# A written order for the first work of all engines: keys and values of group 0 first, then the weight product, and small constants in whole rows

## The chip, the cores and the metric

The kernel runs on one core of a Trainium2 chip. The metric is device time in microseconds (us). A core has five instruction queues that run side by side, each strictly in its own order: TensorE (PE, matmuls and transposes; PEld is its weight load), VectorE (DVE), ScalarE (ACT), GpSimd (POOL), and SyncE (SP), whose queue issues all DMA transfers of this kernel. An instruction waits at the head of its queue until its semaphores are reached, and all that stands behind it waits too.

## The reference, cut to what matters

Two layers over 8 batches of 128 tokens, width 512, all in f32. Layer 0 is a cross-attention with one head, without a mask, followed by a linear layer whose low-rank part is chosen by a gate. Layer 1 is a cross-attention with 32 query heads and 8 key/value groups, and a gated feed-forward network with integer weights. The layers are wired with layer norms and residual sums; `ctx` is the context `ctx_4096`.

```python
# layer 0, attention
Q = einsum('btx,dx->btd', text, Wq) + bq
K = einsum('bpx,dx->bpd', features, Wk) + bk
scores = einsum('btd,bpd->btp', Q, K) / sqrt(512)
attended = einsum('btp,bpd->btd', softmax(scores), features)
# layer 0, linear part with a routed low-rank part (TOPK = 1)
out = einsum('bsd,od->bso', hidden_states, W) + b
scores = x @ gate_w.T + gate_b          # 4 ranks: 8, 16, 32, 64
final = x @ A[:r].T @ B[:, :r].T        # r is the rank that the gate selects
# layer 1, attention: 32 heads, 8 key/value groups, head size 128
q = rmsnorm(x @ q_proj_w.T); k = rmsnorm(ctx @ k_proj_w.T); v = ctx @ v_proj_w.T
# layer 1, feed-forward: integer weights, dequantised by groups of 128
...
```

## The kernel before

**Numbers in two parts.** An f32 operand is split into a rounded high part and the remainder (`_h`, `_l`), and a product takes three matmuls (`mm3`, lines 78 to 80). A split is a cast on ScalarE and a subtraction on VectorE (`split_fast`), a cast on ScalarE and a subtraction on GpSimd (`split_both`), or both on GpSimd (`split_pool`, lines 61 and 62).

**Halves and blocks.** The 1024 tokens are two halves (`hf`) of four blocks of 128 (`HB = 4`). Matrices of 512 rows come in four pieces (`KT = 4`) of 128 x 512.

**Layer 0** does not form Q and K. It forms M = Wq^T Wk once (`weight_product`, 48 matmuls), then per half `proj_T`: the normed tokens times M, four blocks of 12 matmuls into a PSUM pool of two banks (`ps_mm`), each evicted by ScalarE with a bias column `vcol` (line 185). The bias terms need row sums of weight times bias: `vcol` from WkT and `bq`, `ucol` from WqT and `bk`. `ucol` goes to HBM and comes back as a row on all partitions (`u_d`, then `p0T`, lines 366 and 368), where VectorE reduces it (`usum`) and multiplies it with the tokens (line 188). After that come scores (line 232), softmax, the product with the context, a second layer norm, the gate and low-rank part (`ag`, 64 columns of A and 4 of the gate padded to 128, line 278), and the output product with `WT` and `BT`. Both halves run as generators that are advanced in turn.

**Keys and values of layer 1** depend on the context alone: `kv_group(g)` loads group g's weights, splits them and makes four `kv_part`s of 24 matmuls with 256 columns, each followed by Square sums, casts, cuts and a norm; `kv_out` writes them to HBM. Groups 0 to 5 fill TensorE beside layer 0 and before layer 1, groups 6 and 7 go into layer 1's first rounds.

**What sets the order.** All of this stands in the part of the program that a scheduler orders by its own cost estimates. From layer 1's rounds on (line 944) the order is written out by hand. Waits at most eight transfers deep are seen in SyncE's queue: each DMA waits for the one eight before it. The loads at the start are issued in the scheduler's order: Wq and Wk, x, bq, WkT, x, bk, WqT, small constants (lines 375 to 381), the context, and so on. The tables `gsT`, `usT`, `dsT` (lines 918 to 920) are read in pieces of 16 and 56 bytes, the gate's columns in pieces of 16 bytes.

Of the kernel before, what the change touches and what calls it, by code (L numbers as in the profile page):

```python
# [34 lines left out]
def f32(ap):  # L35
    return ap.bitcast(F32)
# [3 lines left out]
def tile_layers(ctx: ExitStack, tc: tile.TileContext, t, out: bass.AP):  # L40
# [36 lines left out]
    def mm3(o, ah, al, bh, bl, start, stop):  # L77
        nc.tensor.matmul(o, ah, bl, start=start, stop=False)  # L78
        nc.tensor.matmul(o, ah, bh, start=False, stop=False)  # L79
        nc.tensor.matmul(o, al, bh, start=False, stop=stop)  # L80
# [88 lines left out]
    gb = w0.tile([P, 4], F32, name="gb")  # L169
    ag = w0.tile([P, KT, P], F32, name="ag")  # L170

    bTh, bTl = (w0.tile([P, D], F32R, name=f"bT_{p}") for p in "hl")
    nc.vector.memset(ag[:, :, 68:128], 0.0)
    scale0 = 1.0 / math.sqrt(D)

    def proj_T(w, src, bias, dst):
        for j in range(KT):
            ps = ps_mm.tile([P, TOK], F32, name="mm")
            cols = slice(j * P, (j + 1) * P)
            for k in range(KT):  # L180
                mm3(
                    ps, w[0][:, k, cols], w[1][:, k, cols], src[0][:, k, :], src[1][:, k, :],
                    k == 0, k == KT - 1,
                )
            nc.scalar.activation(dst[:, j, :], ps, AF.Identity, bias=bias[:, j : j + 1])

    def dot(junk, a, b, o):
        nc.vector.scalar_tensor_tensor(junk, a, 1.0, b, ALU.mult, ALU.mult, accum_out=o)

    def weight_product():  # L190

        wq_, wk_ = wts["WqT"], wts["WkT"]
        pss = [ps_mm.tile([P, D], F32, name="mm") for _ in range(2)]
        pss += [ps_kv.tile([P, 2, 2 * HD], F32, name="kv").rearrange("p a b -> p (a b)") for _ in range(2)]
        for k in range(KT):
            for j, ps in enumerate(pss):
                cols = slice(j * P, (j + 1) * P)
                mm3(
                    ps, wq_[0][:, k, cols], wq_[1][:, k, cols], wk_[0][:, k, :], wk_[1][:, k, :],
                    k == 0, k == KT - 1,  # L200
                )
        mh, ml = (l0.tile([P, KT, D], F32, name="qx", bufs=2).bitcast(F32R) for _ in range(2))
        for j, ps in enumerate(pss):
            split_fast(mh[:, j, :], ml[:, j, :], ps)
        wts["M"] = mh, ml

    def layer0(hf):
        xt = xs[hf]
        xn = layernorm_T(
            hf, ps_tr, keep=lambda b: (mvk[:, hf * HB + b, :], rsk[:, hf * HB + b : hf * HB + b + 1])  # L210
        )
        if hf == 0:
            weight_product()
        yield
        kT = c_st[hf]
        qT = w0.tile([P, KT, TOK], F32R, name="wkf0_" + "hl"[hf]).bitcast(F32)
        proj_T(wts["M"], xn, vcol, qT)
        yield

# [55 lines left out]
        for b in range(HB):  # L275
            cols = slice(b * P, (b + 1) * P)
            for k in range(KT):
                nc.tensor.matmul(
                    agp[:, b, :], xf[:, k, cols], ag[:, k, :], start=(k == 0), stop=(k == KT - 1)
                )  # L280
# [57 lines left out]


    wk_st, wq_st = (l0.tile([P, KT, D], F32, name="qx", bufs=2) for _ in range(2))  # L340
    for k in range(KT):
        rows = slice(k * P, (k + 1) * P)
        nc.sync.dma_start(wq_st[:, k, :], t["Wq"][rows, :])
        nc.sync.dma_start(wk_st[:, k, :], t["Wk"][rows, :])
    for b in range(HB):
        nc.sync.dma_start(xs[0][:, b, :], t["x"][b])
    bq_bc, bk_bc = (l0.tile([P, D], F32R, name=f"cn_{p}", bufs=1).bitcast(F32) for p in "hl")
    wkT_st, wqT_st = (l0.tile([P, KT, D], F32, name="k0T", bufs=2) for _ in range(2))
    nc.sync.dma_start(bq_bc, t["bq"].to_broadcast([P, D]))
    for k in range(KT):  # L350
        nc.sync.dma_start(wkT_st[:, k, :], t["WkT"][k * P : (k + 1) * P, :])
    for k in range(KT):
        for nm, st_ in (("WqT", wq_st), ("WkT", wk_st)):
            split_fast(wts[nm][0][:, k, :], wts[nm][1][:, k, :], st_[:, k, :])
    A, B = layer0(0), layer0(1)
    next(A)
    for k in range(KT):
        dot(wkT_st[:, k, :], wkT_st[:, k, :], bq_bc, vcol[:, k : k + 1])
    for b in range(HB):
        nc.sync.dma_start(xs[1][:, b, :], t["x"][HB + b])  # L360
    nc.sync.dma_start(bk_bc, t["bk"].to_broadcast([P, D]))
    for k in range(KT):
        nc.sync.dma_start(wqT_st[:, k, :], t["WqT"][k * P : (k + 1) * P, :])
        dot(wqT_st[:, k, :], wqT_st[:, k, :], bk_bc, ucol[:, k : k + 1])
    u_d = dram.tile([1, D], F32, name="u_d")
    nc.sync.dma_start(u_d.rearrange("o (k p) -> p (o k)", p=P), ucol)
    u_bc = l0.tile([P, HB, P], F32R, name="p0T").bitcast(F32).rearrange("p b c -> p (b c)")
    nc.sync.dma_start(u_bc, u_d.to_broadcast([P, D]))
    nc.vector.tensor_reduce(usum, u_bc, AX.X, ALU.add)
    c_st = [l0.tile([P, KT, TOK], F32, name="k0T", bufs=2) for _ in range(2)]  # L370
    for hf in range(2):
        for k in range(KT):
            nc.sync.dma_start(c_st[hf][:, k, :], t["ctxT"][k * P : (k + 1) * P, hf * TOK : (hf + 1) * TOK])
            (split_both if hf else split_fast)(cTh[hf][:, k, :], cTl[hf][:, k, :], c_st[hf][:, k, :])
    nc.sync.dma_start(b0, t["ffn_b"].to_broadcast([P, D]))
    nc.sync.dma_start(gb, t["gate_b"].to_broadcast([P, 4]))
    nc.sync.dma_start(ag[:, :, 0:64], t["AT"].rearrange("(k p) r -> p k r", p=P))
    nc.sync.dma_start(ag[:, :, 64:68], t["gwT"].rearrange("(k p) r -> p k r", p=P))
    bs = stage.tile([P, D], F32, name="wstage")
    nc.sync.dma_start(bs[0:64, :], t["BT"])  # L380
    nc.sync.dma_start(bs[64:128, :], t["BT"])
    split_pool(bTh, bTl, bs)
    next(B)
    next(A)
    tile_w0("WT")
    load_w0("WT", split_pool)
    next(B)
    done = False
    order = [A, B]
    while order:  # L390
        for it in list(order):
            try:
                next(it)
            except StopIteration:
                order.remove(it)

    def rms_factor(ssq, n, kind):
# [10 lines left out]
    wkn = const.tile([P, HD], F32, name="wkn")  # L408
    nc.sync.dma_start(wqn, t["qnw"].to_broadcast([P, HD]))
    nc.sync.dma_start(wkn, t["knw"].to_broadcast([P, HD]))  # L410
    nc.vector.scalar_tensor_tensor(wkn, wkn, 1.0 / math.sqrt(HD), wqn, ALU.mult, ALU.mult)
    kT_d, v_d = {}, {}
# [16 lines left out]

    def kv_part(g, hf, b0_):  # L430
        wh, wl = kvw[g]
        if b0_ == 0:
            kvo[g, hf] = (
                kvp.tile([P, HB, HD], F32, name="kn", bufs=1),
                kvp.tile([P, HB, HD], F32R, name="vh"),
                kvp.tile([P, HB, HD], F32R, name="vl"),
            )
        kn, vh, vl = kvo[g, hf]
        ps = ps_kv.tile([P, 2, 2 * HD], F32, name="kv")
        for i in range(2):  # L440
            cols = slice((b0_ + i) * P, (b0_ + i + 1) * P)
            for k in range(KT):
                mm3(
                    ps[:, i, :], cTh[hf][:, k, cols], cTl[hf][:, k, cols], wh[:, k, :], wl[:, k, :],
                    k == 0, k == KT - 1,
                )
        ssq = small.tile([P, 2], F32, name="kssq")
        for i in range(2):
            junk = small.tile([P, HD], F32, name="junk", bufs=2)
            nc.scalar.activation(junk, ps[:, i, 0:HD], AF.Square, accum_out=ssq[:, i : i + 1])  # L450
        bs = slice(b0_, b0_ + 2)
        nc.scalar.copy(vh[:, bs, :], ps[:, :, HD:])
        nc.vector.tensor_tensor(vl[:, bs, :], ps[:, :, HD:], f32(vh[:, bs, :]), ALU.subtract)
        rk = rms_factor(ssq, 2, "k")
        for i in range(2):
            nc.vector.scalar_tensor_tensor(
                kn[:, b0_ + i, :], ps[:, i, 0:HD], rk[:, i : i + 1], wkn, ALU.mult, ALU.mult
            )
# [19 lines left out]

    for g in range(4):
        kv_group(g)  # L480
# [436 lines left out]

    nc.sync.dma_start(sg_sb, t["gsT"].rearrange("(c p) g -> p c g", p=P))
    nc.sync.dma_start(su_sb, t["usT"].rearrange("(c p) g -> p c g", p=P))
    nc.sync.dma_start(sd_sb, t["dsT"].rearrange("(c p) g -> p c g", p=P))  # L920
    for k in range(KT):
# [326 lines left out]
```

## Time and profile before

| what | value |
|---|---|
| median of 3 runs | 849.55 us (848.87 to 850.13) |
| the profiled execution | 851.54 us, span 849.8 us |
| busy: PE, PEld, DVE, ACT, POOL | 816.7, 687.3, 648.1, 514.6, 602.4 us |
| DMA | 167.85 MB, mean 198 GB/s, 155388 packets, 16048 of them under 512 B |
| mean granted TensorE clock | 0.987 of full speed |

The profile shows one execution. Busy time counts from the start of an instruction to its end; matmuls overlap, so a row of 128 x 512 is listed with 0.39 us while one starts every 0.23 us. A row of the timeline has the start, the length, the engine, the line of the code, the operation, `out<-in` by the program's names, shapes, a count, and in brackets the idle time before it with what ended it. `SPq` is SyncE's queue. A row of waits has who waited for whom, the sum in us, how often, and the longest. A row of stretches has the stretch, its length, busy times of PE, PEld, DVE, ACT and POOL with instruction counts, the granted clock of TensorE, the share of DMA engines and GB/s.

### The profile page before, as it was taken

The page shows a single profiled execution, that of the slowest core. Times are in us where ns is not written, and L with a number is a line of the kernel's source. Part 1 is how long each engine was busy: PE and PEld are TensorE (multiplying, and loading weights), DVE is VectorE, ACT ScalarE, POOL GpSimd, SP SyncE. Part 2 cuts the span into 40 slices and gives each one's busy share as a digit, 9 for nine tenths or more (in the row PEclk, how much of TensorE's full clock was granted, in tenths as well). Part 3 has the DMA queues.
Part 4 walks back from the last instruction along what each step waited for, and adds up shares of the span by engine and source line. Part 5 has one row for each costly group of instructions (what it writes and reads, how often), then busy time and mean ns, then how long its engine had stood idle before and what let it go on. Part 6 is the DMA issues. An engine that isn't in the chain of part 4 may idle for free.

```text
span 849.8 us, 14099 instructions
## 1 busy us (share of the span) xinstructions
PE 816.7 (96%) x4264; PEld 687.3 (81%) x4264; DVE 648.1 (76%) x1105; ACT 514.6 (61%) x1687; POOL 602.4 (71%) x615
## 2 busy tenths in 40 slices
PE   6589999999999999999999999999999999999996
PEld 5479999899878888888888888888888866778775
DVE  7843897685677777777777777777798897998987
ACT  4233443245567766676667666677776668765663
POOL 2362784234588877787778778798897778798686
PEclk9789999999999999999999999999999999999998
DMA  9751542073789988888888888988887612232202
GB/s 324 154 149 61 181 148 106 27 241 137 223 287 297 291 273 257 290 256 260 261 272 280 255 258 275 293 270 271 273 256 227 201 36 86 74 87 75 63 25 100
DMA packets 155388, 167.85 MB, mean 198 GB/s; under 512 B 16048, under 2 KB 94640, under 8 KB 155312
## 3 DMA queue, kind: packets, MB, share of 16 engines
q1 hardware_dynamic: 155312, 166.94, 62.0%
q8 instruction: 34, 0.56, 0.3%
q14 instruction: 42, 0.34, 0.2%
HBM read 107.66 MB, written 59.25 MB: 196 GB/s over the span
## 4 chain that ended last, share of the span: by engine, by line
PE 80%; DMA 7%; DVE 4%; issue 3%; POOL 3%; ACT 2%; SPq 1%; POOLq 0%; DVEq 0%; ACTq 0%
PE mm L78 8%; PE mm L80 8%; PE mm L79 8%; PE f L1017 7%; PE o L679 7%; PE f L1018 7%; PE o L680 6%; PE o L682 6%; PE s L610 6%; PE kv L80 3%; PE kv L79 3%; PE kv L78 3%; PE o L659 2%; PE o L658 2%; PE o L660 2%
## 5 line engine op out<-in xcount | busy, mean ns | idle before, releaser
L624 ACT ACTIVATE pr<-s,nm 128x128 f32<-128x128 f32 x256 | 90.6, 366 | 47.6 <-DVE nm L618 45.8
L78 PE MATMUL mm<-wq_l,xnT_h 128*128 128x512 f32 x288 | 118.7, 412 | 0.2 <-DVE q L579 0.2
L80 PE MATMUL mm<-wq_h,xnT_l 128*128 128x512 f32 x288 | 113.8, 395 | 0.0
L79 PE MATMUL mm<-wq_h,xnT_h 128*128 128x512 f32 x288 | 113.5, 394 | 0.0
L651 POOL TENSOR_TENSOR pT_l<-pT,pT_h 128x512 fp32r<-128x512 f32 x64 | 83.0, 1296 | 26.6 <-ACT pT_h L650 26.3
L679 PE MATMUL o<-wo_l,aT_h 128*128 128x512 f32 x256 | 101.3, 396 | 0.3 <-DVE xs L687 0.3
L680 PE MATMUL o<-wo_h,aT_h 128*128 128x512 f32 x256 | 100.3, 392 | 0.0
L632 POOL TENSOR_TENSOR pr<-pr,rs 128x512 f32<-128x512 f32 x64 | 67.8, 1059 | 25.4 <-DVE rs L630 25.1
L636 DVE STREAM_TRANSPOSE pb<-pr 128x512 f32<-128x512 f32 x64 | 45.5, 711 | 48.2 <-POOL pr L632 48.1
L570 ACT ACTIVATE junkq<-mm 128x128 f32<-128x128 f32 x256 | 71.8, 280 | 10.9 <-PE mm L80 4.8
L78 PE MATMUL kv<-wkv_l,cT_h 128*128 128x256 f32 x256 | 73.1, 286 | 0.0
L79 PE MATMUL kv<-wkv_h,cT_h 128*128 128x256 f32 x256 | 73.1, 286 | 0.0
L80 PE MATMUL kv<-wkv_h,cT_l 128*128 128x256 f32 x256 | 73.1, 286 | 0.0
L610 PEld LDWEIGHTS s<-kT,qT 128*128 128x128 f32 x512 | 66.8, 191 | 5.5
L708 POOL TENSOR_TENSOR qT<-qT,q 128x512 fp32r<-128x512 f32 x42 | 54.3, 1292 | 23.8 <-ACT qT L707 23.8
L682 PE MATMUL o<-wo_h,aT_l 128*128 128x512 f32 x256 | 69.0, 391 | 0.0
L401 POOL TENSOR_TENSOR rrq<-msq,nhalf 128x4 f32<-128x4 f32 x64 | 64.6, 1009 | 5.3
L610 PE MATMUL s<-kT,qT 128*128 128x128 f32 x512 | 67.3, 274 | 0.0
L664 ACT CAST aT_h<-o 128x512 fp32r<-128x512 f32 x64 | 37.6, 587 | 48.0 <-PE o L660 47.7
L80 PEld LDWEIGHTS mm<-wq_h,xnT_l 128*128 128x128 f32 x288 | 54.1, 188 | 12.6
L78 PEld LDWEIGHTS mm<-wq_l,xnT_h 128*128 128x128 f32 x288 | 54.5, 189 | 10.0 <-ACT junkq L570 0.4
L79 PEld LDWEIGHTS mm<-wq_h,xnT_h 128*128 128x128 f32 x288 | 54.4, 189 | 9.9
(264 smaller groups left out, 2417.1 us busy)
## 6 DMA issues: line engine op xcount, KB each, us to landing
q_d<-qb SPq DMA_DIRECT2D x64, 256.0 KB, 4.2
qT<-q_d SPq DMA_DIRECT2D x64, 256.0 KB, 4.1
p_d<-pb SPq DMA_DIRECT2D x64, 256.0 KB, 2.5
pT<-p_d SPq DMA_DIRECT2D x64, 256.0 KB, 4.6
wst<-in_qpT SPq DMA_DIRECT2D x36, 256.0 KB, 3.9
wst<-in_opT SPq DMA_DIRECT2D x36, 256.0 KB, 3.1
wkv<-in_kvT SPq DMA_DIRECT2D x8, 512.0 KB, 4.0
v_d<-vh SPq DMA_DIRECT2D x16, 256.0 KB, 2.9
```

The costliest lines, as they stand in the source:

```text
L78: nc.tensor.matmul(o, ah, bl, start=start, stop=False)
L79: nc.tensor.matmul(o, ah, bh, start=False, stop=False)
L80: nc.tensor.matmul(o, al, bh, start=False, stop=stop)
L401: nc.gpsimd.tensor_tensor(r[:, :n], ms[:, :n], nhalf[:, :n], ALU.pow)
L570: nc.scalar.activation(junk, qps[u][:, r * HD : (r + 1) * HD], AF.Square, accum_out=ssq[:, r : r + 1])
L610: nc.tensor.matmul(sp[:, r, :], qTs[u][:, r, :], kTt[blocks[j]][:, :, i, :], start=True, stop=True)
L624: nc.scalar.activation(pr[:, r, :], sps[u][:, r, :], AF.Exp, bias=nms[u][:, r : r + 1], accum_out=sm[:, r : r + 1])
L632: nc.gpsimd.tensor_tensor(pr, pr, rs.unsqueeze(2).to_broadcast([P, NQ, P]), ALU.mult)
L651: nc.gpsimd.tensor_tensor(pl, tps[u], f32(ph), ALU.subtract)
L679: nc.tensor.matmul(po, ah[:, r, :], wl, start=r == 0, stop=False)
L680: nc.tensor.matmul(po, ah[:, r, :], wh, start=False, stop=False)
L682: nc.tensor.matmul(po, al[:, r, :], wo[wset[j], r][0], start=False, stop=r == NREP - 1)
```

## The change

The first part of the program leaves the scheduler and is written in order for every queue (`tc.manual_schedule()`); what comes after it is still ordered by the scheduler, which may put later instructions between those of the written part.

- Group 0's weights and context half 0 are loaded first, piece by piece, and four blocks of keys and values are summed side by side in four banks (three of `ps_kv`, one of `ps_s`). Their evictions (`kv_part` with banks given) come after the first block of the weight product.
- `weight_product` becomes `product(j, ks)`, one output block after the other, with cuts, norms and transposes of half 0 written between them. Two of Wk's cuts move from VectorE to GpSimd.
- The row sums for `vcol` and `ucol` (one VectorE instruction each before) become a GpSimd product (`times`) and a ScalarE sum (`column`).
- Keys and values of group 1 for half 0 start before the first projection. The cuts of context half 1 are written between the projection's evictions. Loads are issued in the written order; `b0`, `gb`, `ag`, `BT`, `WT` come after it.
- `ag` has 68 columns instead of 128 and comes as one table with whole rows; the scale tables `gsT`, `usT`, `dsT` come as whole rows too.

```diff
-    ag = w0.tile([P, KT, P], F32, name="ag")
+    ag = w0.tile([P, KT, 68], F32, name="ag")
...
-                    agp[:, b, :], xf[:, k, cols], ag[:, k, :], start=(k == 0), stop=(k == KT - 1)
+                    agp[:, b, 0:68], xf[:, k, cols], ag[:, k, :], start=(k == 0), stop=(k == KT - 1)
...
-    for k in range(KT):
-        dot(wkT_st[:, k, :], wkT_st[:, k, :], bq_bc, vcol[:, k : k + 1])
...
+    def times(w_st, b_bc, k):
+        nc.gpsimd.tensor_tensor(w_st[:, k, :], w_st[:, k, :], b_bc, ALU.mult)
+
+    def column(w_st, col, k):
+        nc.scalar.activation(w_st[:, k, :], w_st[:, k, :], AF.Identity, accum_out=col[:, k : k + 1])
+
+    with tc.manual_schedule():
+        w0_st = kvw[0] = kvp.tile([P, KT, 2 * HD], F32, name="wkv", bufs=1)
+        for k in range(KT):
+            nc.sync.dma_start(w0_st[:, k, :], t["kvT"][0][k * P : (k + 1) * P, :])
+            load_c(0, k)
...
+        banks = [ps_kv.tile([P, 2, 2 * HD], F32, name="kv")[:, 0, :] for _ in range(3)]
+        banks.append(ps_s.tile([P, HB, P], F32, name="s")[:, 0:2, :].rearrange("p a b -> p (a b)"))
+        for k in range(KT):
+            split_fast(wh[:, k, :], wl[:, k, :], w0_st[:, k, :])
+            split_fast(cTh[0][:, k, :], cTl[0][:, k, :], c_st[0][:, k, :])
+            for b, ps in enumerate(banks):
+                cols = slice(b * P, (b + 1) * P)
+                mm3(ps, cTh[0][:, k, cols], cTl[0][:, k, cols], wh[:, k, :], wl[:, k, :], k == 0, k == KT - 1)
+        kv_load(1)
...
+            split_fast(wq_[0][:, k, :], wq_[1][:, k, :], wq_st[:, k, :])
+            (split_both if k > 1 else split_fast)(wk_[0][:, k, :], wk_[1][:, k, :], wk_st[:, k, :])
...
+        product(0, range(KT))
+
+        nc.vector.scalar_tensor_tensor(wkn, wkn, 1.0 / math.sqrt(HD), wqn, ALU.mult, ALU.mult)
+        for b0_ in (0, 2):
+            kv_part(0, 0, b0_, banks[b0_ : b0_ + 2])
+        stats(0)
+        stats(1)
+        product_cut(0)
+        product(1, range(KT))
...
+        for k in range(KT):
+            column(wkT_st, vcol, k)
+        kv_out(0, 0)
+        for b in range(HB):
+            stats(HB + b)
+        kv_part(1, 0, 0)
...
+        for k in range(KT):
+            times(wqT_st, bk_bc, k)
+            column(wqT_st, ucol, k)
+        normed(HB)
+        normed(HB + 1)
+
+        def second_context(k):
+            split_both(cTh[1][:, k, :], cTl[1][:, k, :], c_st[1][:, k, :])
+
+        proj_T(wts["M"], xnT0[0], vcol, qTs0[0], second_context)
+        nc.sync.dma_start(u_d.rearrange("o (k p) -> p (o k)", p=P), ucol)
...
+        nc.sync.dma_start(u_bc, u_d.to_broadcast([P, D]))
+        turns(HB + 2)
+        turns(HB + 3)
+    proj_T(wts["M"], xnT0[1], vcol, qTs0[1])
+    nc.vector.tensor_reduce(usum, u_bc, AX.X, ALU.add)
+    A, B = layer0(0), layer0(1)
+    nc.sync.dma_start(b0, t["ffn_b"].to_broadcast([P, D]))
+    nc.sync.dma_start(gb, t["gate_b"].to_broadcast([P, 4]))
+    nc.sync.dma_start(ag, t["agT"].rearrange("p (k r) -> p k r", r=68))
...
+    split_pool(bTh, bTl, bs)
+    tile_w0("WT")
+    load_w0("WT", split_pool)
...
+    kv_part(1, 0, 2)
+    kv_out(1, 0)
...
-    nc.sync.dma_start(sg_sb, t["gsT"].rearrange("(c p) g -> p c g", p=P))
+    nc.sync.dma_start(sg_sb, t["gsT"].rearrange("p (c g) -> p c g", g=KT))
...
-        "gsT": g["L1_ffn_gate_s"].T,
+        "gsT": g["L1_ffn_gate_s"].reshape(KT, NI, P).transpose(2, 1, 0).reshape(P, NI * KT),
```

## The prediction

> **What bounds the kernel now.** I read the page first, then TensorE's waits, then the queues of the stage in which it waits.
>
> ```profile
> PE 816.7 (96%) x4264; PEld 687.3 (81%) x4264; DVE 648.1 (76%) x1105; ACT 514.6 (61%) x1687; POOL 602.4 (71%) x615
> ...
> PE   6589999999999999999999999999999999999996
> ```
>
> TensorE is busy in 96% of the span, and the slices that are not full are the first three (64 us). From 60 us on its matmuls follow each other at 0.23 us (512 columns), 0.12 us (256) and 0.11 us (f32, 128). So the time is TensorE's work plus the time that it loses, and nearly all loss is at the start. Its waits in the first 260 us:
>
> ```profile
> PE tr L100 <- DVE xnT_l L107: 7.5, 2, 5.0
> PE mm L78 <- ACT wkf_h L185: 6.5, 2, 6.0
> PE mm L78 <- DVE wkf_l L66: 5.6, 1, 5.6
> ```
>
> To these comes a slow clock after each pause: the stretches show the granted clock behind the busy times.
>
> ```profile
> 20.00:30.00 10.00, 3.06 (x15) 2.17 (x16) 10.00 (x24) 3.25 (x6) 2.38 (x7) 0.64 1.04 275
> ...
> 40.00:50.00 10.00, 5.51 (x14) 4.35 (x15) 0.00 (x0) 2.72 (x5) 2.80 (x3) 0.66 0.60 157
> ```
>
> Counted: up to 38.5 us TensorE did 72 matmuls of 512 columns, 32 transposes and 3 of 256 columns, 16.4 + 3.5 + 0.4 = 20.3 us of work. It goes on at 44.49 us, so 24.2 us are lost; the next 12 matmuls take 5.3 us, not 2.7 (half clock), then 0.45 us of wait and some tenths more: **28.0 us lost by 70 us**, and nothing after that up to 200 us. Who is late is in the DMA queue:
>
> ```profile
> 29.06 0.38 SPq L918 DMA_DIRECT2D sg_sb<-in_gsT  x1
> 29.77 2.99 SPq L919 DMA_DIRECT2D su_sb<-in_usT  x1
> 32.81 1.37 SPq L920 DMA_DIRECT2D sd_sb<-in_dsT  x1
> 34.27 0.45 SPq L366 DMA_DIRECT2D u_d<-ucol  x1
> 34.77 1.93 SPq L373 DMA_DIRECT2D k0T<-in_ctxT  x4
> 36.80 2.17 SPq L74 DMA_DIRECT2D wstage<-in_WT  x2
> 43.07 2.07 SPq L368 DMA_DIRECT2D p0T<-u_d  x1
> ```
>
> The scale tables and u_d are some 4,600 pieces of 4 to 56 bytes; the moved bytes drop from about 300 GB/s to 5 to 44 GB/s between 32.8 and 42.4 us (2.1 ns a piece). Context half 1 lands behind them, ScalarE stands in its queue at that cast, and the eviction that frees TensorE's bank stands behind the cast.
>
> **The change, step by step.** Work on TensorE is the same but for L278. So I compare lost time at two places. The order of instructions in the built kernel shows which queue stands where; durations are rows of the trace before.
>
> *Start.* The first matmul waits for a 128 KB and a 256 KB load and their casts in place of two 256 KB ones: about 4.7 us against 5.55. 48 key and value matmuls (5.7 us, at half clock for about 4 us: 2 lost) lie over the arrival of Wq and Wk. The last of these is the 18th load: 3.8 MB at 345 KB/us (317 fit the loads landed by 29 us, 365 the stretch from 10 to 20 us), 11.0, plus the 2.9 us that one v_d transfer takes from issue to landing: 13.9; then ScalarE 0.62 and GpSimd 1.29, so the first product block ends near 16.6 us with 8.4 us of work done, 8.2 lost. Waits for the first cut (about 1.4) and for transposes (0.9) make 10.5. Before the third block of the first projection TensorE has 96 x 0.119 + 72 x 0.228 + 16 x 0.11 = 29.6 us of work, so it gets there at **40.1 us**.
>
> *The new wait.* That block needs the bank of the first one, freed by ScalarE's eviction. In ScalarE's queue four row sums of Wq's columns stand ahead of it; each waits for GpSimd's product with bk. In GpSimd's queue the splits of BT and of two WT pieces stand ahead of these, and those loads are the last of 45 units of 256 KB: 11.8 MB / 345 = 34.2, plus 2.9: the second WT piece lands at 37.1 us, the first at 36.4. GpSimd from there: 0.62 + 1.3 + 0.6 + 0.2 + 0.62 + 1.3 + 0.7 = 5.3, then four products at 1.29 (the row of the same form below): 47.0.
>
> ```profile
> 53.87 1.29 POOL L62 TENSOR_TENSOR wq_l<-wstage,wq_h 128x512 fp32r<-128x512 f32 x1
> ```
>
> ScalarE's last sum 0.78, eviction 0.68 and a tenth: TensorE goes on at **48.6 us**, 8.5 us late, and at half clock again (2.5, as after the wait of 6.0 before).
>
> *The round trip of u.* The sums are done at 47.8. VectorE's queue holds its reduction of u ahead of all cuts of half 1.
>
> ```profile
> DVE usum L369 <- DMA p0T<-u_d: 13.1, 1, 13.1
> ```
>
> u_d took 8.7 us and the broadcast 8.6 behind other loads; alone the nearest rows are 2.9 plus 512 x 2.1 ns, 4.0, and 3.3 for the broadcast. Bounds together: 5.8 to 17.3; I take 7.3, since the queue is nearly empty then. 55.1; VectorE 0.6 + 6 x 0.68 + 0.5: 60.3; a context load (its stage buffer is freed by these) 2.8; GpSimd 0.62 + 0.6 + 1.3 + 1.29: **66.9 us**, when the last context cut that the next key block needs is there. TensorE's work by then is 29.6 + 11.5 (24 x 0.228, 32 x 0.11, 21 x 0.119) = 41.1, so it has lost 25.8. Against 28.0: **2.2 us gained**.
>
> *The switch of layers.* Group 0 and half of group 1 are used up at the start, so less is left to cover the end of layer 0. Before, TensorE has over 110 key and value matmuls (13 us) between the last output block of layer 0 (174.3 us) and the queries. In the changed order 19 remain. After that last block VectorE has, up to the last query weight: one add 0.6, three normalisations 1.6, statistics 0.7, three cuts 1.8, four weight cuts 2.4, zero points 0.5, value cut and two keys 0.9, a group's weight cuts 1.4, small waits 0.3: 10.2 us. TensorE has 19 x 0.119 + 16 x 0.11 + 9 x 0.228 = 6.1. Lost: 4.1, and the clock. After a pause of 2.55 us at 19 us, eight transposes took 1.43 us, not 1.03: 0.4. **4.5 us lost** (2.5 to 6).
>
> The Trainium skill, "TensorE: Matmul & The Clock Gate", section "Why this matters for your kernels", warns of idle gaps over about 3 us, after which the array runs at half clock. By it the long wait above is charged and this gap of 2 to 3 us is not; the 0.4 would go and the time would be 851.2.
>
> *The rest.* L278 takes 68 columns in place of 128 in 32 matmuls of 0.11: 0 to 1.7 us less. The 256-column row costs 0.12 and the f32 one of 128 columns 0.11, so columns alone do not set the pitch: I take 0.3. The whole-row tables free the DMA stretch above, which is in the start already; nothing else waits for them. The Square, copy and cut of the first values in four pieces, the moved wkn product and the memset lie on ScalarE and VectorE beside TensorE's product: 0 as long as TensorE has the second product block, up to 1 if not (in the 10.5).
>
> *Sum:* -2.2 + 4.5 - 0.3 = **+2.0 us**. The profiled execution took 851.54 us (span 849.8), the median of three runs is 849.55, 2.0 lower; on the profiled one this gives 853.5, on the median **851.6 us**. About 0.2% (1.7 us) is what a measurement here can tell from no change.
>
> **The rivals.**
> 1. *Faster: the switch is covered.* If the queries' weights are cut before VectorE meets the last half's normalisations, only the start counts: 849.55 - 2.2 - 0.3 = 847.1; and if the loads also run at 365 KB/us (TensorE goes on 1.9 us earlier), 845.2. For it: before, there is no loss at the switch at all. Against: VectorE's order is fixed and holds a group's weight cuts ahead of the last query cut. It decides if those 10.2 us become under 6.
> 2. *Slower by the u round trip.* If u_d and its broadcast take 8.7 + 8.6 as before, everything behind VectorE's reduction comes 10 us later: 861.6. For it: u_d still moves 4-byte pieces. Against: the loads that stood ahead of it are gone. From 4 us more it decides (over 855).
> 3. *The start's gain is kept whole:* if BT and WT land before 31 us, the wait at the third block is 2 to 3 us in place of 8.5 and the time 845 to 846. That needs 420 KB/us, above all rows.
>
> **How the numbers follow.** My case 0.6 (own range 848.5 to 855, since the switch is 2.5 to 6, the round trip moves it by 2 and L278 by 1.4), rival 1 0.25, rival 2 0.1, rival 3 0.05. Range for 8 in 10: 845 to 857, which takes in rival 1 and the shorter half of rival 2. Slower by over 0.2%: 0.42 of my case and rival 2, 0.52; within: 0.17 of my case and 0.03 of rival 1, 0.20; faster: the rest, 0.28.
>
> **What would show it.** Right: TensorE waits 7 to 10 us for ScalarE's eviction near 40 us; GpSimd's products of Wq wait for WT; VectorE waits for the broadcast of u until 53 to 58 us; waits for VectorE of 3 to 5 us near 185 us. Wrong: no wait at 40 us (the loads were faster), none at 185 us, or a wait over 5 us near 64 us (rival 2).

## The result and the profile after

The changed kernel took **864.19 us** (863.67 to 866.11, four runs), the kernel before 849.21 us beside it: a ratio of 1.0179 (1.0161 to 1.0197), 15 us slower. Measured again beside the experiments (e13 below) it was 1.0175. Foretold were 851.6 us, between 845 and 857. The sign of the likeliest case was right, the size was not. The profiled execution took 866.11 us, with a span of 864.3 us.

The page of the changed kernel, the busy line and TensorE's slices:

```profile
PE 824.4 (95%) x4264; PEld 691.1 (80%) x4264; DVE 641.5 (74%) x1088; ACT 517.8 (60%) x1705; POOL 611.7 (71%) x625
...
PE   6957999998999999999999999999999999999996
```

Before, the first three slices were not full. Now slices 1, 3 and 4 (to 86 us) are not, and the tenth (194 to 216 us) has an 8. These are the two places of the forecast, the start and the switch of layers. TensorE's waits up to 260 us say for whom it stands there:

```profile
PE mm L78 <- ACT wkf_h L184: 8.0, 1, 8.0
PE kv L80 <- POOL cT_l L70: 7.0, 2, 6.4
PE kv L78 <- ACT cT_h L65: 4.5, 1, 4.5
PE mm L78 <- DVE wq_l L635: 2.3, 1, 2.3
```

The third row is the first matmul (foretold 4.7 us; 5.5 in e13). The first is the foretold wait for ScalarE's eviction (7 to 10 us). The second is the one that the forecast named as the sign of rival 2, a wait of over 5 us near 64 us. The rows of the timeline on its way:

```profile
51.61 0.38 SPq L537 DMA_DIRECT2D u_d<-ucol  x1
62.20 0.32 SPq L544 DMA_DIRECT2D p0T<-u_d  x1
65.33 0.69 DVE L548 TENSOR_REDUCE usum<-p0T 128x1 f32<-128x512 f32 x1 [16.86 <-DMA p0T<-u_d]
66.13 1.88 POOL L200 TENSOR_SCALAR tm<-mvk,usum 128x4 f32<-128x4 f32 x2 [6.88 <-DVE usum L548]
67.98 1.26 POOL L70 TENSOR_TENSOR cT_l<-k0T,cT_h 128x512 fp32r<-128x512 f32 x1
69.29 0.80 PE L80 MATMUL kv<-wkv_h,cT_l 128*128 128x256 f32 x2 [6.42 <-POOL cT_l L70]
```

`u_d` is issued at 51.61 us into a queue that holds nothing else, and the broadcast that reads it cannot go before 62.20. Then VectorE reduces it; GpSimd's `tm`, which needs that sum, stands ahead of the context cut in GpSimd's queue; and TensorE needs the cut. So TensorE goes on 7.1 us after u_d has landed.

The same count as in the prediction (time minus work at 0.2275, 0.119 and 0.11 us a matmul) shows where the 15 us are:

| lost by | 40 us | 80 us | 200 us | 220 us | 300 us |
|---|---|---|---|---|---|
| before | 19.7 | 28.1 | 29.0 | 29.7 | 32.4 |
| changed | 14.2 | 34.6 | 35.4 | 42.1 | 45.1 |

The new order is 5.5 us ahead at 40 us, 6.5 behind at 80, and loses 6.0 more than before at the switch (6.7 against 0.7). From 220 to 300 us the two lose nearly the same (3.0 and 2.7). Counted at the same matmul instead of the same time, they are 6.5 us apart after 160 us of work, 13.0 after 180, still 13.0 after 500, and 14.6 at the last matmul. The 1.6 us at the end are in this trace alone: in the second trace of the changed kernel (e13) the distance is 6.4, 13.3, 12.9 and 13.3 us. So the start and the switch, 6.5 us each, are nearly the whole loss.

### The profile page after: what moved, and what is told of

Its sections match the earlier page's. It is cut to its first block, busy times and chain, and to the rows that moved or that the text cites. A ratio compares the mean times of both kernels' runs of the same rounds, so it can differ in the third digit from the quotient of the medians.

```text
span 864.3 us, 14101 instructions
## 1 busy us (share of the span) xinstructions
PE 824.4 (95%) x4264; PEld 691.1 (80%) x4264; DVE 641.5 (74%) x1088; ACT 517.8 (60%) x1705; POOL 611.7 (71%) x625
## 4 chain that ended last, share of the span: by engine, by line
PE 70%; DMA 8%; POOL 8%; DVE 6%; ACT 3%; issue 3%; SPq 1%; POOLq 0%; ACTq 0%; DVEq 0%
PE mm L78 7%; PE mm L80 7%; PE mm L79 7%; PE f L1113 7%; PE f L1114 6%; PE o L775 5%; PE o L776 5%; PE o L778 5%; PE s L706 5%; DMA pT<-p_d 3%; PE kv L80 3%; PE kv L79 3%; PE kv L78 3%; PE o L756 1%; PE o L755 1%
## 5 line engine op out<-in xcount | busy, mean ns | idle before, releaser
L804 POOL TENSOR_TENSOR qT<-qT,q 128x512 fp32r<-128x512 f32 x42 | 54.2, 1291 | 22.7 <-ACT qT L803 22.5
L746 ACT CAST pT_h<-pT 128x512 fp32r<-128x512 f32 x64 | 39.8, 622 | 43.4 <-DMA pT<-p_d 42.1
```

## The experiments

The kernel before took 851.0 to 851.4 us beside these runs, so kernels are compared by their ratio to it. Diffs are against the kernel named.

| run | edit | us | ratio (95%) |
|---|---|---|---|
| e13_after_again | changed kernel again | 865.74 | 1.0175 (1.0156 to 1.0193) |
| e1_tables | before + whole-row tables | 851.28 | 1.0000 (0.9989 to 1.0011) |
| e3_before_u16 | before + u in pieces of 16 B | 843.57 | 0.9907 (0.9892 to 0.9921) |
| e2_u16 | changed + u in pieces of 16 B | 856.76 | 1.0068 (1.0042 to 1.0095) |
| e5_wt_late | changed + WT late | 859.30 | 1.0104 (1.0087 to 1.0120) |
| e14_products_first_only | changed + products first | 857.13 | 1.0070 (1.0052 to 1.0089) |
| e4_norms_late | changed + norm weights late | 864.14 | 1.0150 (1.0134 to 1.0166) |
| e10_cut_late | changed + last group's cuts late | 862.07 | 1.0131 (1.0116 to 1.0146) |
| e6_fill | changed + a block moved to the switch | 871.74 | 1.0247 (1.0229 to 1.0264) |
| e7_three_edits | changed + u, WT, cuts | 847.93 | 0.9968 (0.9957 to 0.9978) |
| e11_products_first | e7 + products first | 843.56 | 0.9923 (0.9904 to 0.9942) |
| e12_products_first_norms_late | e11 + norm weights late | 842.23 | 0.9907 (0.9888 to 0.9926) |
| e8_before_u16c | before + u in 16 B, read in that order | 842.99 | 0.9911 (0.9898 to 0.9925) |
| e9_before_u16c_tables | e8 + whole-row tables | 851.36 | 1.0006 (0.9995 to 1.0017) |

### The write of u: e3, e2, e1

In the first two runs one line changes, in the kernel before and in the changed one; each partition then writes its four values side by side. In these two runs u comes back permuted and the dot product does not know of it, which leaves the result as it was only because the bias is zero here; e7 and e8 below read it in the right order.

```diff
-nc.sync.dma_start(u_d.rearrange("o (k p) -> p (o k)", p=P), ucol)
+nc.sync.dma_start(u_d.rearrange("o (p k) -> p (o k)", p=P), ucol)
```

> The kernel before, with only u_d written in the order in which the partitions hold it, 128 pieces of 16 bytes in place of 512 of 4 bytes (so u is read back permuted; both bias vectors are zero here). Theory A (u_d's 4-byte pieces are the slow ones): u_d lands in 3 to 5 us after the tables, context half 1 about 5 us earlier, TensorE's wait at 44 us nearly gone; time 843 to 845. Theory B (the tables are): u_d lands about 1 us earlier, 848 to 849.5.

> The changed kernel, with only u_d written in 128 pieces of 16 bytes (u is read back permuted; both bias vectors are zero). Theory A (the round trip of u is what was mis-sized): u_d lands in 3 to 5 us in place of 10.6, VectorE's reduction starts near 58 us, TensorE's wait of 6.4 us at 69 us falls to 0 to 2; time 857 to 859. Theory B (that wait comes from GpSimd's order, the WT splits ahead of the context cuts): the wait stays over 4 us, time 862 to 864.

The third leaves u alone and gives the kernel before the whole-row tables and the 68 gate columns.

```diff
-nc.sync.dma_start(su_sb, t["usT"].rearrange("(c p) g -> p c g", p=P))
+nc.sync.dma_start(su_sb, t["usT"].rearrange("p (c g) -> p c g", g=KT))
```

> The kernel before, with only the whole-row tables (ag of 68 columns from one table; gsT, usT, dsT in whole rows); the order of the work stays the scheduler's. Theory A (the 512 pieces of 4 bytes of u_d hold the DMA queue for most of the 32.8 to 42.4 us stretch): u_d still lands 8 to 10 us after its issue, context half 1 about 3 us earlier than before, TensorE's wait of 6.0 us shrinks to about 3.5; time 846 to 847. Theory B (the tables' pieces of 16 and 56 bytes hold it, as the prediction priced them): the wait is gone, u_d lands in about 4 us; time 841 to 843. L278 with 68 columns adds 0 to -1.7 us in both.

The list of DMA issues gives bytes and median time from issue to landing; the first fence is the changed kernel, the second e2, the third e1.

```profile
u_d<-ucol SPq DMA_DIRECT2D x1, 2.0 KB, 10.6
```

```profile
u_d<-ucol SPq DMA_DIRECT2D x1, 2.0 KB, 2.5
```

```profile
u_d<-ucol SPq DMA_DIRECT2D x1, 2.0 KB, 9.0
```

The same 2 KB take 10.6 us in 512 pieces and 2.5 in 128. The 384 pieces more cost 8.1 us, 21 ns each, ten times the 2.1 ns that the prediction took from the stretch with the tables. That stretch was mostly u_d's own: in the trace before, the last table landed at 36.1 us (issued at 32.81, 3.3 us) and u_d at 43.0 (issued at 34.27, 8.7 us). And e1 shows that these 8.7 us were not the tables' doing: with them in whole rows, u_d still takes 9.0 us.

The time of e1 says less. Both theories foretold less than the 851.3 us that it took. And the edit does more than it seems: with the new tables the scheduler writes another order of the work, on every engine the one of e9 below, so e1 is not the kernel before with other tables alone.

In e2 the loss by 80 us falls from 34.6 to 27.1 us, in e3, whose order is the one before, from 28.1 to 20.5. So the price of u was in both kernels, 0.9 to 1.1% of the time. The waits of e3's TensorE have only this left of the 6.5 us for that eviction:

```profile
PE mm L78 <- ACT wkf_h L185: 0.6, 1, 0.6
```

### GpSimd's order: e5 and e14

e5 writes the loads and splits of BT and WT behind the second half's transposes. e14 leaves those and u alone, and writes the products of Wq's columns ahead of the second half's statistics.

```diff
@@ e5
         turns(HB + 3)
+        bs = stage.tile([P, D], F32, name="wstage")
+        ...
+        split_pool(bTh, bTl, bs)
+        tile_w0("WT")
+        load_w0("WT", split_pool)
@@ e14
+        for k in range(KT):
+            times(wqT_st, bk_bc, k)
         for b in range(HB):
             stats(HB + b)
         kv_part(1, 0, 0)
...
         for k in range(KT):
-            times(wqT_st, bk_bc, k)
             column(wqT_st, ucol, k)
```

> The changed kernel, with the loads and splits of BT and WT written behind the second half's transposes, so that they stand behind the products of Wq's columns in GpSimd's queue. Theory A (the 8.0 us wait of TensorE for ScalarE's eviction near 44 us is GpSimd's queue: 0.62 + 0.62 + 1.28 + 0.62 + 1.27 = 4.4 us of splits ahead of the four products): the products start near 41 us in place of 45.5, the wait becomes 3 to 4 us, u and all behind it come 4.4 us earlier, and the time is 864.2 - 4.4 = 859 to 861. Theory B (the products wait for their loads, or ScalarE for something else): the wait stays at 7 to 8 us and the time at 863 to 866. Theory C (the later WT is then what the feed-forward of layer 0 waits for): the wait near 44 us falls, and a new one for WT's pieces stands between 75 and 110 us; 862 to 866.

> The changed kernel with one edit: the products of Wq's columns written ahead of the second half's statistics, and so ahead of the splits of BT and WT too, in GpSimd's queue; u still goes out in 512 pieces of 4 bytes. Theory A (the order of GpSimd's queue is the cause, and u's pieces cost much only because they start at 51.6 us, when TensorE has nothing left to do): u is written at about 40 us, its broadcast is read at about 54, 11 us earlier; TensorE's wait of 8.0 us is gone and the one of 6.4 us is under 2 us: 10 to 13 us less than the changed kernel, 852 to 855. Theory B (u's pieces cost their 10 us wherever they start, because TensorE runs out of work earlier too): the waits move to 47 to 58 us and the gain is the 8.0 us wait at most, 857 to 860.

GpSimd's queue in the changed kernel, before the edits:

```profile
36.75 0.19 POOL L87 TENSOR_SCALAR rsk<-mvk 128x1 f32<-128x1 f32 x1 [4.92 <-DVE mvk L86]
...
39.33 0.62 POOL L61 TENSOR_SCALAR bT_h<-wstage 128x512 fp32r<-128x512 f32 x1
...
45.53 5.30 POOL L433 TENSOR_TENSOR xnT_l<-xnT_l,cn_l 128x512 f32<-128x512 f32 x4
```

It stands 4.92 us for VectorE's statistics, to 36.75, computes factors from them, and only at 39.33 us takes the splits that the prediction had it take from 36.4 us on, when their loads land. GpSimd waits for no load between 25 and 60 us. In e5 the products start at 39.60 in place of 45.53, TensorE's wait for the eviction falls from 8.0 to 3.9 us, and 0.7% is won: theory A, with the time at the lower end of its range. In e14 they start at 30.87, that wait is gone, and 1.05% (9 us) is won. But u still leaves in 512 pieces (SyncE's queue and TensorE's waits of e14):

```profile
39.49 0.38 SPq L538 DMA_DIRECT2D u_d<-ucol  x1
...
50.18 0.32 SPq L545 DMA_DIRECT2D p0T<-u_d  x1
```

```profile
PE kv L78 <- DVE kn L375: 9.0, 1, 9.0
```

12 us earlier, u_d holds its broadcast back for the same 10.7 us, and TensorE stands 9.0 us, now for keys that VectorE makes with a factor that GpSimd computes behind `tm`. Theory B holds: u's pieces cost their time wherever they start. Two costs therefore lie one after the other, GpSimd's order (9 us) and u's pieces (9 us by e2), and neither is the cause of the other.

### What comes ahead of Wq: e4

Two small loads (qnw, knw) move behind those of Wq and Wk.

```diff
-        nc.sync.dma_start(wqn, t["qnw"].to_broadcast([P, HD]))
-        nc.sync.dma_start(wkn, t["knw"].to_broadcast([P, HD]))
         for k in range(KT):
             ...
             nc.sync.dma_start(wk_st[:, k, :], t["Wk"][rows, :])
+        nc.sync.dma_start(wqn, t["qnw"].to_broadcast([P, HD]))
+        nc.sync.dma_start(wkn, t["knw"].to_broadcast([P, HD]))
```

> The changed kernel, with the two broadcasts of the norm weights (qnw, knw) issued after Wq and Wk instead of ahead of them. Theory A (these two, 128 pieces of 512 bytes each from one row, cost the queue about 2 us and so Wq lands 3 us late): Wq's first piece lands near 9.5 us, TensorE has lost about 11 us at 30 us in place of 13; but the wait near 44 us is set by GpSimd and the queue, so it grows by most of that: time 862 to 864. Theory B (the start decides the rest): the whole 2 to 3 us are kept, 861 to 862. Theory C (Wq is late for the plain bytes ahead of it): no change in Wq's arrival beyond 0.5 us, 864.

ScalarE's first cast of Wq starts at 9.78 us in place of 11.88 (10.36 in e13), and 9.1 us are lost by 20 us in place of 11.6 (10.0 in e13). Theory A had the wait for the eviction take this back. It does not: it is 8.0 us long as before and ends at 50.16 us in place of 52.21 (50.92 in e13). The round trip of u takes it back. u_d takes 11.8 us in place of 10.6 (11.4 in e13), its broadcast goes out 0.9 us earlier only, and behind it TensorE stands 9.8 us, to 73.47. By 80 us 34.3 us are lost, as in the changed kernel (34.6, and 34.5 in e13). The ratio is 0.25% below e13's with intervals that overlap, so whether it gains 2 us elsewhere or nothing stays open.

### The switch of layers: e10 and e6

The switch in the changed kernel, the stretches and then rows of TensorE's and VectorE's timeline:

```profile
200.00:210.00 10.00, 6.96 (x36) 5.12 (x36) 8.82 (x20) 5.61 (x16) 1.97 (x4) 0.85 0.91 263
210.00:220.00 10.00, 10.00 (x59) 9.27 (x58) 3.74 (x7) 4.66 (x23) 3.33 (x5) 0.81 0.53 196
```

```profile
205.75 0.68 DVE L635 TENSOR_TENSOR wq_l<-wst,wq_h 128x512 fp32r<-128x512 f32 x1
206.35 1.42 DVE L66 TENSOR_TENSOR wkv_l<-wkv,wkv_h 128x256 fp32r<-128x256 f32 x4
...
208.29 0.68 DVE L635 TENSOR_TENSOR wq_l<-wst,wq_h 128x512 fp32r<-128x512 f32 x1
```

```profile
206.49 0.51 PE L78 MATMUL mm<-wq_l,xnT_h 128*128 128x512 f32 x1 [2.28 <-DVE wq_l L635]
...
208.52 1.09 PE L100 MATMUL tr<-ident,xn 128*128 128x128 f32 x4 [0.76 <-DVE xnT_l L107]
```

TensorE waits for the third query cut; then the last group's four weight cuts stand ahead of the fourth. From 206.49 to 213.86 us it does work of 6 x 0.2275 + 4 x 0.11 + 15 x 0.119 = 3.6 us in 7.37 us, of which 0.76 is a wait: 3.0 us go to the clock (granted 0.85 and 0.81 in the two stretches, 0.50 from 207.0 to 213.8 us).

e10 writes those cuts one round later. e6 moves a block of 24 key and value matmuls ahead of the first queries, and so out of a later round.

```diff
@@ e10
+        at(-6, "kv0", kv_cut, NG - 1)
         for n, parts in zip(range(-7, -2), ((0, 1, 2), (3,), (4,), (5,), (6,))):
...
-        at(-7, "kv0", kv_cut, NG - 1)
@@ e6
-        for n, parts in zip(range(-7, -2), ((0, 1, 2), (3,), (4,), (5,), (6,))):
+        for n, parts in zip(range(-7, -2), ((0, 1, 2, 3), (4,), (5,), (6,), ())):
```

> The changed kernel, with the four weight cuts of the last group (VectorE, 1.42 us together, and ScalarE's four casts) one round later, so that they no longer stand ahead of the last query cut. Theory A (at the switch of layers TensorE waits for VectorE's queue): the gap between the third and fourth step of the first query falls, 1.4 to 2.1 us are won at 200 to 220 us and nothing is lost elsewhere: 862 to 863. Theory B (the query weights wait for their loads, which begin at 198 us when layer 0's last product is done): the switch still loses 6 to 7 us and the time stays within 1 us of 864.2. Theory C (the group's keys are then late in the next round): 865 or more.

> The changed kernel, with one more block of 24 key and value matmuls (24 x 0.119 = 2.9 us) of the last groups written ahead of the first queries, and so one less in the rounds behind them; the work is the same. Theory A (the loss at the switch is missing cover: TensorE has too little other work while layer 0's last output becomes the first query): by 200 us 2 to 3 us less are lost, and since the rounds behind then lack the block, 2 to 4 us more are lost between 210 and 300 us; 863 to 866. Theory B (the loss is a chain that runs however much work stands there, or the clock): no change at either place, 864 within 1 us. Theory C (the cover is missing only here, the later rounds have enough): 861 to 862.

e10: the wait falls from 2.3 to 1.3 us, the loss from 200 to 220 us from 6.7 (7.1 in e13) to 5.2, and the ratio by 0.0044 (0.0010 to 0.0077 by the two intervals). That is theory A; of the 3.7 us that the ratio gives, the trace shows 1.5 to 1.9 at this place. e6: from 200 to 210 us 2.0 us are lost in place of 4.9, as theory A said. But the time, 871.7 us, is above every theory's range. The next block now comes before its own weights are cut; VectorE's cuts stand behind a transpose that waits for a write of the keys:

```profile
214.39 0.71 DVE L385 STREAM_TRANSPOSE kT<-kn 128x512 f32<-128x512 f32 x1 [4.09 <-DMA kT_d<-kT]
215.03 1.39 DVE L66 TENSOR_TENSOR wkv_l<-wkv,wkv_h 128x256 fp32r<-128x256 f32 x4
```

```profile
215.46 0.58 PE L78 MATMUL kv<-wkv_l,cT_h 128*128 128x256 f32 x1 [6.51 <-DVE wkv_l L66]
```

From 220 to 300 us, where the block is missing, 6.3 us are lost in place of 3.0. So the cover is missing at the first queries, and the later rounds have none to spare; that the moved block would come before its own weights, the larger part of the price, no theory had.

### The base: e13

> The changed kernel once more, as a base for the single edits, beside the same kernel before. If its ratio to before is 1.018 as in the first result, the base is 866 to 867 us where before takes 851.3, and each edit's gain is read from ratios (e.g. the late norm weights 0.3%, the late cut 0.5%). If it takes 864.2 whatever before takes, the gains are those of the medians (0 and 2.1 us).

865.74 us beside 851.19, ratio 1.0175: the first case. 34.5 us are lost by 80 us and 42.3 by 220, as in the first trace (34.6 and 42.1).

### Together, and versions that beat both: e7, e11, e12, e8, e9

e7 is the changed kernel with u in 16-byte pieces, WT late and the cuts late. There the dot product reads the broadcast in the permuted order. e11 adds the products ahead of the statistics, e12 the late norm weights.

```diff
-            dot(w, xt[:, b - hf * HB, :], u_bc, trow[:, b : b + 1])
+            dot(
+                w.rearrange("p (k c) -> p k c", k=KT), xt[:, b - hf * HB, :].rearrange("p (k c) -> p k c", k=KT),
+                u_bc.rearrange("p (c k) -> p k c", k=KT), trow[:, b : b + 1],
+            )
```

> The changed kernel with three edits: u_d written in 128 pieces of 16 bytes and the dot product reading the broadcast in that permuted order (same result), BT and WT behind the products, the last group's cuts one round later. If the three costs are separate places they add up: 864.2 - 7.4 (measured for the pieces alone) - 4.4 - 1.5 to 2 = 850.5, within 1 us of the kernel before. If the 16-byte pieces and the GpSimd order are two ways to shorten one chain that something else then bounds, less: 853 to 856.

> The changed kernel with the three edits of the earlier run (16-byte pieces, BT and WT late, last group's cuts one round later; 847.9), and the products of Wq's columns written ahead of the second half's statistics in GpSimd's queue. In that earlier run GpSimd stood 4.92 us for VectorE's statistics, to 35.2 us, and the products came behind the four, at 39.7 to 45.1 us; TensorE waited 3.9 us for the eviction. Theory A (the 3.9 us and the half clock after it are GpSimd's order): the products run at about 31 to 36.5 us, the wait is under 1 us, and the time 842 to 844. Theory B (TensorE then waits for the context of half 1 or for u instead): 846 to 848.

> The same, with qnw and knw loaded behind Wq and Wk. In the changed kernel this made the first product block 2 us earlier and the time no better. Theory A (it was lost in the wait behind GpSimd's queue, which does not move with it): with that wait gone the gain is kept, 1 to 2 us below the run with the products first. Theory B (the 2 us were not on the path in any case): the same time within 0.5 us.

e7 won somewhat more than its parts were expected to give (847.9 against 850.5). By the ratios to e13's the parts add up: 1.07 (e2), 0.71 (e5) and 0.44% (e10), together 2.2, and e7 lies 2.1% below it. e11's products run from 31.41 to 36.9 us, TensorE's wait for the eviction is gone, and 843.6 us is theory A. e12 has 12.5 us lost by 70 us where e11 has 14.6, and 1.3 us less time; that is theory A's size, though the intervals overlap, and e4's trace puts the loss there at u and not at GpSimd's queue. On the page of e12 the start has only its first slice left, and the switch (168 to 189 us) one of 8:

```profile
PE   6999999989999999999999999999999989999996
```

The same edit of u in the kernel before, then with the tables:

> The kernel before, with u_d written in 128 pieces of 16 bytes, and the dot product of layer 0 reading the broadcast in that permuted order by a strided view (same result as before). If the strided read costs VectorE nothing that counts: 843 to 844, as with the pieces alone. If it takes VectorE twice as long (8 x 0.65 us more, in a stage where TensorE's next key block waits for VectorE): 845 to 849.

> The kernel before with u_d in 128 pieces of 16 bytes (dot product in the permuted order, same result) and the constants in whole rows. If the tables count for nothing, as they did alone: 843.0 within 1 us. If they only did not count because u_d held the queue behind them: 841 to 842.

e8 is at 843.0, although its dot products took 1.08 us in place of 0.68 (medians): VectorE had the time. **e9 is at 851.4, and neither theory had that.** With the tables the scheduler writes another order, on every engine that of e1. VectorE's groups between 36 and 44 us, e8 and then e9:

```profile
L66 DVE TENSOR_TENSOR wkv_l<-wkv,wkv_h 128x256 fp32r<-128x256 f32 x4 | 1.4, 409 | 0.0
```

```profile
L66 DVE TENSOR_TENSOR wkv_l<-wkv,wkv_h 128x256 fp32r<-128x256 f32 x4 | 4.5, 1182 | 0.0
```

In e9 the four weight cuts run beside four context cuts of GpSimd (35.71 to 41.31 us) and take three times as long. The load that reuses their buffer goes out at 42.37 us in place of 38.62, ScalarE stands 7.2 us for it with TensorE's evictions behind, and TensorE waits 2.1 us for ScalarE and 3.2 for VectorE; by 60 us 27.5 us are lost, in e8 19.4. In e1, with the same order but a slow u_d, the context lands later, the four cuts take 415 ns each, and that load goes out at 39.41 us; e1 loses its time to u instead. So e1 and e9 differ by u alone (its write and the order of its read) and take the same time, and neither says what the tables cost without the new order. The chain is read from the traces; no run has this order with a fast u and without the overlap, so it is argued, not shown. The Trainium skill, "SBUF — State Buffer", section "Who interferes with whom", says that a VectorE instruction with two SBUF inputs contends with a GpSimd instruction that reads SBUF. These cuts have two such inputs, and 1182 against 409 ns agrees with it.

The best version of the new order (e12, 0.9907) and of the old one (e8, 0.9911; e3, 0.9907) are equal within their intervals: five edits bring the one where a single edit brings the other.

## Why the prediction was right or wrong

**The step that failed most: the round trip of u.** The sum took 4.0 + 3.3 us, "2.9 plus 512 x 2.1 ns". Measured: 10.6 + 3.1. The bounds held it (5.8 to 17.3), but the value was taken from a stretch in which tables were read and u_d was written (and in which 201 GB/s moved from 35.8 to 36.8 us, not 5 to 44), and the 8.7 us of the trace before were put down to the queue. Nothing else was in the queue now, and it took longer. What the sum puts behind the round trip was right: from VectorE's reduction (65.33 us) to the last context cut (77.3) 12.0 us pass, foretold 11.8. TensorE stood earlier, though, from 62.88 us, for the third cut behind `tm`, and then ran at half clock; neither was in a term. With u near the foretold price (2.5 + 3.5 us in e2) the start ends near the forecast, with 27.1 us lost by 80 us against 25.8. Rival 2 named the mechanism, at a chance of 0.1; "the loads that stood ahead of it are gone" was true and shortened the broadcast alone (8.6 to 3.1).

**The wait at 44 us.** Place, size (8.0 us against 8.5) and most of the chain were right (splits of WT, products, sums, eviction), and e5 and e14 confirm it. One link was not: GpSimd did not wait for the loads of WT. It stood for VectorE's statistics to 36.75 us and worked on them to 39.33, which was in no term, so the wait ended at 52.2 us, not 48.6.

**The start.** 14.2 us lost by 40 us (13.1 in e13), not 10.5. Wq's first cast was at 11.88 us (10.36 in e13) behind two small broadcasts that the sum counted by their bytes alone. In e4 it is at 9.78, and the trace shows the loss by 80 us unchanged.

**The switch.** Place and mechanism were right (19 matmuls do not cover VectorE's chain), the size was 6.7 us and not 4.5. The clock was priced at 0.4 us, from a gap of 2.55 us at 19 us; here 3.0 us went to it after a wait of 2.28. That gap was a poor measure. The clock fell behind it too (granted 0.50 from 22.7 to 33.0 us), but only when the eight transposes were nearly over, and half of the slow stretch lay under the next wait, 5.0 us long. The Trainium skill's section "Why this matters for your kernels" ("TensorE: Matmul & The Clock Gate") puts the loss behind idle gaps of over about 3 us; here the slow clock followed a shorter single gap, and in e10 two gaps of 1.34 and 1.12 us, so the measurement decides, and the smaller price that the prediction gave for that rule was further off than its own.

**L278 and the tables** were priced at 0.3 and 0 us; e1 gives both together, with the scheduler's other order, as no change (0.11% either way). The trace lists 64 matmuls of L278, not 32, so the sum's own upper bound would have been 3.3 us, not 1.7.

The sum, redone against before at the same matmul: +6.5 us at the start in place of -2.2, +6.5 at the switch in place of +4.5, nothing for L278 in place of -0.3. That is 11.0 of the 12.6 us between 851.6 and 864.2; the rest is what the first trace loses late and e13's does not.

## What to carry to other kernels

Price a small DMA by its number of pieces from a row of the same kind, written or read, and ask of a long small transfer whether it is slow by itself before blaming the queue: one edit of its layout answers that. Where a scheduler orders the work, compare the order on each engine before reading the time of an edit: e1 and e9 came with another one. An order written by hand is only as good as each engine's queue: list what stands ahead of the first instruction on the path, also the engine that this queue will stand for. And work that is moved to the front to fill one hole is missing at the next, so count the cover that is left at every later switch.

## What the runs showed of the hardware

- A write of 512 pieces of 4 bytes to HBM took 10.5 to 11.8 us with nothing else in the queue (u_d in the changed kernel, e13, e10, e6 and e4), and 8.6 to 9.0 us in e5, e1 and the kernel before. 128 pieces of 16 bytes took 1.4 to 2.9 us (e2, e3, e7, e8, e11, e12), and 4.1 in e9.
- VectorE's 128 x 256 subtraction took 0.41 us with GpSimd mostly idle (e8) and 1.18 us beside GpSimd's subtractions (e9); a dot product of 128 x 512 took 0.68 us, and 1.08 with one operand read at a stride of 16 bytes (e8, medians).
- TensorE's clock was at half from 207.0 to 213.8 us after a single wait of 2.28 us (changed kernel), and from 206.8 to 210.2 us after waits of 1.34 and 1.12 us (e10).
